# A graph layer on one core: the source table's rows made inside the first level's steps, the node layer in one matmul per batch with its inputs fetched at the batch's own step

## The chip, the cores and the metric

The kernel runs on one core of one Trainium2 chip. A core has five engines with queues of their own: TensorE (PE in the profile, with its weight loads as PEld), VectorE (DVE), ScalarE (ACT), GpSimd (POOL) and SyncE (SP), which here only issues transfers. The metric is the device time of one execution in microseconds. Three executions of the kernel before took 2367.4, 2370.09 and 2371.28 us; the median is 2370.09 us.

## The reference, cut to what matters

```python
h = relu(layernorm(x))                                   # x: 12500 nodes x 64
e = silu(concat(h[src], h[dst], w) @ eW1 + eb1)          # 212500 edges x 128, dst is sorted
e = silu(e @ eW2 + eb2)
agg = segment_sum(e, src, 12500)                         # 12500 x 128
out = x + silu(concat(h, agg) @ nW1 + nb1) @ nW2 + nb2   # 12500 x 64
```

The sum goes over `src`, while the list is sorted by `dst`. `h[src] @ eW1[:64]` is a row of a table A, with one row of 128 numbers per node, and `h[dst] @ eW1[64:128]` a row of a table B. `h @ nW1[:64]` is called the own rows' part of the node layer below.

## The kernel before, in words

The 12500 nodes stand in 100 buckets of 125, and four buckets are a batch (25 batches). The 212500 edges come in 208 blocks of 1024.

**Feed.** `normed` makes h, `turned` transposes four buckets of it (tile `hr`), and `products` multiplies them by both halves of eW1 (`product`, L246, L250, L253: matmul, copy on ACT, difference on DVE, since every table row is kept as a rounded half and a rest). Table A goes to DRAM as `ta` (tile `rows_a`), table B as `tb` (tile `got`), and the turned rows as `hd`. The feed is a list of small pieces, handed out between other work.

**Sends.** For every block the B rows of its 1024 edges are picked by matmul (L493) from a window of `tb`, copied on ACT into `qs` (L505, eight buffers) and scattered to DRAM rows in `q` by eight indirect transfers on POOL (L515), four for each half block. The rows' places come from counting on DVE (L426, L434, L451, L453) and PE (L439, L463, in the PSUM tile `misc`); `picked` (L415) makes the selection matrix.

**Levels.** Each bucket's rows of `q` are filled in ranks. When the blocks up to a level's end are scattered, its ranks are full in every bucket, and a level of 25 batches can run; there are 14 levels, and the last needs all blocks. A step (512 edges; one step to a batch in the first two and the last eight levels, two in the others) is: `one` on DVE (L644, which node each edge has), its transpose (L601, L606), the rows of `q` and A added (L615, L622) and SiLU (L631), the second layer (L655, L661, L665), the sum over nodes (L675) and its addition to `aggT` (L684 or L686). A batch's `qt` (rows of `q`) is fetched four batches ahead (L569) and its `a` (rows of `ta`) three ahead (L589), both on SP's queue; the first `qt` of a level waits for the scatters.

**Node layer.** In the last level `nodes` follows each batch in four parts, one at each free place of the step after: four z matmuls (two on the sums, L312; two on the turned rows, L315) and SiLU (L317); four matmuls into `o` (L321); the sum with x into `os` on DVE (L324); the store (L326 through the helper at L126). Its inputs `xr` (L126, and an addition on POOL, L300) and `hrn` (L302) are issued with the batch's `qt`, four batches ahead. `os` and `zs` have two buffers each, the inputs six.

**Order.** PE, DVE, ACT and SP run in the order in which the code is written. `turn` is the list of a step's parts with four places (None) between, at which a planner (numbers PLAN_...) puts pieces of sends and the feed, to keep scatters ahead of POOL. The first eight blocks go out before that loop, with four pieces of the feed to each piece of a block; then 39 pieces of blocks with three pieces of the feed each; then the loop over the steps.

Of the kernel before, what the change touches and what calls it, by code (L numbers as in the profile page):

```python
# [50 lines left out]
G = 4  # L51
# [13 lines left out]
PLAN_AHEAD, PLAN_ROOM = 30.0, 36.0  # L65
# [14 lines left out]
def tile_gnn(ctx: ExitStack, tc: tile.TileContext, x, src, dst, ew, eW1, eb1, eW2, eb2, nW1, nb1, nW2, nb2, out):  # L80
# [112 lines left out]
    nodes_i = const.tile([P, L], I32, name="nodes_i")  # L193
# [3 lines left out]
    diff = const.tile([P, P], I32, name="diff")  # L197
# [3 lines left out]
    for a in range(2):  # L201
        half = slice(a * D, (a + 1) * D)
        nc.gpsimd.dma_start(w1[half, :, :], eW1[: 2 * D, :].rearrange("(s k) f -> k s f", s=2))
    same = const.tile([P, 1], F32, name="same")
# [33 lines left out]
    def product(s, hr, ps, tag, to):  # L238
# [13 lines left out]
        for a in range(2):  # L252
            nc.vector.tensor_tensor(to[:, a, 1], abs_[a], to[:, a, 0], op=OP.subtract)  # L253

    hd = dram.tile([P, NB // 2, P], F32, name="hd")
    bkt = const.tile([P, 2 * TB, NP], BF16, name="bkt")
# [39 lines left out]
    def nodes_in(B, sb):  # L296
# [4 lines left out]
        hr = sb.tile([P, G // 2, P], F32, name="hrn")  # L301
        nc.sync.dma_start(hr, hd[:, b // 2 : b // 2 + G // 2, :])  # L302
        return xr, hr

    def nodes(B, xr, hr, ps, sb, tag):

        b = B * G

        zs = sb.tile([P, 2, G // 2, L], F32, name="zs")
        z = [ps.tile([P, G // 2, L], F32, name="z", tag=tag) for _ in range(2)]  # L310
        for a in range(2):
            nc.tensor.matmul(z[a], w1g, aggT[:, b + a : b + G : 2, :], start=True, stop=False)  # L312
        for a in range(2):
            half = slice(a * D, (a + 1) * D)
            nc.tensor.matmul(z[a], w1n[half, :], hr[half, :, :L], start=False, stop=True)  # L315
        for a in range(2):
            nc.scalar.activation(zs[:, a], z[a], AF.Silu, bias=nb1c)  # L317
        yield
        o = ps.tile([L, G, D], F32, name="o", tag=tag)
        for t in range(G):  # L320
            nc.tensor.matmul(o[:, t, :], zs[:, t % 2, t // 2, :], w2n, start=True, stop=True)  # L321
        yield
        os_ = sb.tile([L, G, D], F32, name="os")
        nc.vector.tensor_tensor(os_, o, xr, op=OP.add)  # L324
        yield
# [9 lines left out]
    with ExitStack() as work:  # L335
# [8 lines left out]
        misc = sgp.tile([P, 2 * NB + L], F32, name="misc")  # L344
        upto, numbers, spots = misc[:, :NB], misc[:, NB : 2 * NB], misc[:, 2 * NB :]
        nc.tensor.matmul(upto, before, none, start=True, stop=True)
# [131 lines left out]

        def send(s):
# [56 lines left out]
        def send_all(s0, s1):  # L536

            for s in range(s0, s1):
# [5 lines left out]
                for j, _ in enumerate(itertools.zip_longest(send(s), count(s + 1))):  # L544
                    if s + 1 == nblocks and j == 1:
                        counted(s)
# [573 lines left out]
```

## Time and profile before

| what | value |
|---|---|
| median of three executions | 2370.09 us |
| the profiled execution | 2367.31 us, span 2365.5 us |
| busy: PE, PEld, DVE, ACT, POOL | 2028.7, 1902.7, 1814.7, 1333.0, 1655.9 us |
| mean granted clock of TensorE | 0.892 |
| scatters | 1661, mean 973 ns |
| moved by the transfers | 572.83 MB |

A row of the timeline gives the start (us from the span's start), the busy time, the engine, the line, the operation and its tiles, how many are merged, and in brackets how long the engine had been idle and what ended that. An engine with a trailing q is its queue: SPq rows are transfers being issued. A row of the windows gives the stretch, its length, and for each engine the busy time with the number of instructions, then the granted clock of TensorE as a share of full speed, the busy share of the transfer engines and GB/s.

### The profile page before, as it was taken

How to read it: one execution, taken by the hardware profiler on the slowest of the kernel's cores; microseconds unless marked ns; L12 is line 12 of the kernel's file. 1: busy time of each engine (PE TensorE's matmuls, PEld its weight loads, DVE VectorE, ACT ScalarE, POOL GpSimd, SP SyncE). 2: the span in 40 equal slices, each digit the busy share in tenths (PEclk: the TensorE clock that was granted, in tenths of full speed). 3: DMA queues.
4: the chain of work that ended last, by engine and by line, in shares of the span. 5: the costliest groups of instructions: out<-in, count | busy, mean ns of one | idle time of the engine just before them, and what ended most of it. 6: DMA issues, size and time to landing. Idle time of an engine off the chain costs nothing.

```text
span 2365.5 us, 47589 instructions
## 1 busy us (share of the span) xinstructions
PE 2028.7 (86%) x16818; PEld 1902.7 (80%) x16818; DVE 1814.7 (77%) x2865; ACT 1333.0 (56%) x2966; POOL 1655.9 (70%) x1724
## 2 busy tenths in 40 slices
PE   4667798952599779969995999999999999989997
PEld 2455697942499669959995999999999999989885
DVE  8899788885488868886886888888888888875221
ACT  3334464631277547737773777666666666656542
POOL 5777777777777777777777777777777777776110
PEclk9655597965699879979996999999999999999998
DMA  5566797964488647867884888888888888878662
GB/s 161 188 235 231 268 298 248 324 225 133 155 297 263 224 170 250 264 197 255 288 286 143 284 280 265 268 276 271 285 267 291 274 275 277 272 244 277 196 196 85
DMA packets 239835, 572.83 MB, mean 242 GB/s; under 512 B 46756, under 2 KB 99072, under 8 KB 239177
## 3 DMA queue, kind: packets, MB, share of 16 engines
q1 hardware_dynamic: 155283, 390.76, 51.5%
q0 software_dynamic: 54112, 124.65, 14.4%
q10 hardware_dynamic: 30196, 54.31, 7.3%
q8 instruction: 136, 2.23, 0.4%
q14 instruction: 108, 0.88, 0.1%
HBM read 356.61 MB, written 212.87 MB: 241 GB/s over the span
## 4 chain that ended last, share of the span: by engine, by line
PE 58%; DMA 12%; DVE 11%; POOL 6%; issue 4%; ACT 2%; SPq 2%; POOLq 0%; DVEq 0%; ACTq 0%
PE seg L675 15%; PE p L661 14%; PE pt L622 10%; DMA q<-qs,to 8%; PE pt L615 6%; POOL q L515 6%; PE qp L493 6%; PE lr L601 4%; DMA out_dram<-os 3%; DVE each L434 1%; DVE oh L426 1%; PE bc L379 1%; DVE rank L453 1%; DVE terms L451 1%; DVE pick L415 1%
## 5 line engine op out<-in xcount | busy, mean ns | idle before, releaser
L515 POOL DMA_INDIRECT q<-qs,to x1661 | 1616.1, 973 | 526.5 <-issue 396.9
L631 ACT ACTIVATE e<-pt 128x512 f32<-128x512 f32 x450 | 268.7, 597 | 496.2 <-PE pt L622 495.2
L675 PE MATMUL seg<-one,e 128*128 128x125 f32 x3600 | 502.3, 283 | 2.0 <-DVE aggT L686 1.7
L661 PE MATMUL p<-w,e 128*128 128x128 f32 x3600 | 498.6, 282 | 0.0
L661 PEld LDWEIGHTS p<-w,e 128*128 128x128 f32 x3600 | 449.9, 195 | 9.9 <-issue 9.2
L675 PEld LDWEIGHTS seg<-one,e 128*128 128x128 f32 x3600 | 444.2, 193 | 9.4 <-issue 4.9
L622 PE MATMUL pt<-oneT,a 125*128 125x128 f32 (+1 forms) x2800 | 423.0, 289 | 14.4 <-DMA a<-ta 8.5
L493 PEld LDWEIGHTS qp<-win,pick 128*128 128x128 f32 x1664 | 268.5, 224 | 202.6 <-ACT qs L505 121.6
L493 PE MATMUL qp<-win,pick 128*128 128x256 f32 x1664 | 347.7, 340 | 93.5 <-ACT qs L505 60.6
L505 ACT COPY qs<-qp 128x512 f32<-128x512 f32 x418 | 245.1, 587 | 323.9 <-DMA q<-qs,to 222.9
L622 PEld LDWEIGHTS pt<-oneT,a 125*128 125x128 f32 x2800 | 356.8, 194 | 18.3 <-issue 9.7
L644 DVE TENSOR_TENSOR one<-misc,qt 128x500 f32<-128x500 f32 x450 | 302.4, 672 | 78.1 <-PE seg L675 42.1
L686 DVE TENSOR_TENSOR aggT<-aggT,seg 128x500 f32<-128x500 f32 x325 | 218.4, 672 | 185.9 <-PE seg L675 182.2
L434 DVE TENSOR_REDUCE each<-oh 128x100 bf16<-128x800 bf16 x208 | 321.0, 1543 | 7.2
L615 PE MATMUL pt<-ident,qt 128*128 128x128 f32 x1800 | 276.3, 277 | 10.4 <-ACT qs L505 10.1
L606 ACT CAST oneT<-lr 125x512 fp32r<-125x512 f32 x450 | 265.5, 590 | 13.2 <-PE lr L601 13.2
L665 ACT ACTIVATE e<-p 128x512 f32<-128x512 f32 x450 | 268.7, 597 | 6.1 <-PE p L661 6.1
L655 ACT COPY p<-b2f 128x512 f32<-128x512 f32 x450 | 267.2, 594 | 0.0
L451 DVE TENSOR_TENSOR terms<-oh,misc 128x800 f32<-128x800 bf16 x208 | 203.6, 979 | 38.2 <-PE misc L439 38.2
L615 PEld LDWEIGHTS pt<-ident,qt 128*128 128x128 f32 x1800 | 215.3, 144 | 19.7 <-ACT qs L505 11.0
L453 DVE TENSOR_REDUCE rank<-terms 128x8 f32<-128x864 f32 x208 | 219.0, 1053 | 7.2
L426 DVE TENSOR_TENSOR oh<-misc,bkt 128x800 bf16<-128x800 f32 (+1 forms) x209 | 203.8, 975 | 2.4 <-ACT bkt L831 2.4
(153 smaller groups left out, 1653.4 us busy)
## 6 DMA issues: line engine op xcount, KB each, us to landing
a<-ta SPq DMA_DIRECT2D x350, 512.0 KB
qt<-q SPq DMA_DIRECT2D x250, 288.0 KB
qt<-q SPq DMA_DIRECT2D x100, 576.0 KB
q<-zeros ACTq DMA_DIRECT2D x25, 1080.0 KB
q<-qs,to POOLq DMA_INDIRECT x1661
win<-tb SPq DMA_DIRECT2D x208, 120.0 KB
tb<-got SPq DMA_DIRECT2D x30, 512.0 KB
q<-zeros ACTq DMA_DIRECT2D x20, 720.0 KB
```

Source lines behind the costliest of these rows:

```text
L434: nc.vector.tensor_reduce(each, oh.rearrange("p t b -> p b t"), AX.X, OP.add)
L493: nc.tensor.matmul(qp[:, t % 2, :k], halves(pick[:, t * P : (t + 1) * P]), halves(win[:, :k, v]), start=v == 0, stop=v == 1,)
L515: ins = nc.gpsimd.indirect_dma_start(out=q[:], out_offset=bass.IndirectOffsetOnAxis(ap=to[:k, j : j + 1], axis=0), in_=qs[:k, t % 2, a, :] ...
L606: nc.scalar.copy(halves(oneT), st[k].pop("lr"))
L615: nc.tensor.matmul(pt[:, t, :], qt[:, j, :H], ident, is_transpose=True, start=t == 0, stop=False, skip_group_check=True)
L622: nc.tensor.matmul(pt[:, cols, :], halves(a[:L, b, i * H : (i + 1) * H]), halves(oneT[:, cols, :]), start=False, stop=i == 1, skip_group_c ...
L631: nc.scalar.activation(e1, pt, AF.Silu)
L644: nc.vector.tensor_tensor(one.rearrange("p (b j) l -> p b j l", j=n), spots[:, None, None, :].to_broadcast(wide), loc[:, tiles[0][1] : til ...
L655: nc.scalar.copy(p2, b2f)
L661: nc.tensor.matmul(p2[:, t, :], e1[:, t, :], w2, start=False, stop=t == G - 1, skip_group_check=True)
L665: nc.scalar.activation(e2, p2, AF.Silu)
L675: nc.tensor.matmul(item[2][:, b, :], e2[:, t, :], one[:, t, :], start=j < G, stop=j >= G * (n - 1))
```

## The change

1. The feed makes no table A. `hd` is stored earlier in a group, and table B's tile has three buffers to itself. Six pieces of a group become four, and the first eight blocks get three pieces of the feed to each piece of a block.
2. In the first level a batch's `a` is not loaded. `made_a` loads the four buckets' turned rows from `hd` (128 KB), waits three free places, makes A straight into the tile `a` and stores it to `ta` for the later levels. It also makes the own rows' part (two matmuls, two copies on ACT) and stores it to a new DRAM tensor `own` (250 KB a batch).
3. The planner takes 2.6 us more for each step of the first level.
4. The node layer has one z matmul over 500 columns. It accumulates onto the own rows' part, which is copied by DVE into `misc`, the counters' PSUM tile, no longer needed then. In the last level `one` reads the node numbers from SBUF, since `misc` is overwritten.
5. `xr` and the own rows' part (`zo`) are issued at the batch's own step instead of four batches ahead, with five buffers; `zs` and `os` have three. The first `qt` of the last level is issued three batches ahead instead of four, two at once.
6. After the last step the parts left are written in an order of their own (`ending`). The check for irregular input (`flagged`) is computed after the last block, not after the node layers.

```diff
-        z = [ps.tile([P, G // 2, L], F32, name="z", tag=tag) for _ in range(2)]
...
+        if bank is not None:
+            nc.tensor.matmul(bank, w1g, sums, start=False, stop=True, skip_group_check=True)
+            nc.scalar.activation(zsv, bank, AF.Silu, bias=nb1c)
...
         os_ = sb.tile([L, G, D], F32, name="os")
         nc.vector.tensor_tensor(os_, o, xr, op=OP.add)
+        for more in then:
+            nc.vector.tensor_copy(bank, more())
...
-            while B not in done_a:
-                next(feed)
             a = lda.tile([P, G, 2 * H], F32, name="a")
-            nc.sync.dma_start(a, ta_buckets[:, B * G : B * G + G])
+            if c == 0:
+                making[B] = made_a(B, a)
+                next(making[B])
+            else:
+                nc.sync.dma_start(a, ta_buckets[:, B * G : B * G + G])
...
+        def made_a(B, a):
...
+            hr = late.tile([P, G // 2, P], F32, name="hrl")
+            nc.sync.dma_start(hr, hd[:, B * G // 2 : (B + 1) * G // 2, :])
+            for _ in range(3):
+                yield
+            yield from product(0, hr, mm, "mm", a.rearrange("p g (k h) -> p g k h", k=2))
+            yield
+            nc.sync.dma_start(ta_buckets[:, B * G : B * G + G], a)
+            zo = [mm.tile([P, G // 2, L], F32, name="zo", tag="mm") for _ in range(2)]
+            for h in range(2):
+                half = slice(h * D, (h + 1) * D)
+                nc.tensor.matmul(zo[h], w1n[half, :], hr[half, :, :L], start=True, stop=True)
+            zos = late1.tile([P, G * L], F32, name="zos")
+            for h in range(2):
+                nc.scalar.copy(zos.rearrange("p (i a l) -> p i a l", a=2, l=L)[:, :, h], zo[h])
+            yield
+            nc.sync.dma_start(own[:, B, :], zos)
...
+            if c == len(LEVELS) - 1:
+                node_in[B] = nodes_in(B, ndp[0])
             if g == n - 1:
-                fetch(c * (NB // G) + B + NQ)
+                i = c * (NB // G) + B
+                while len(fetched) <= i + NQ and (len(fetched) < final or i + 3 >= final):
+                    fetched.append(0)
+                    fetch(len(fetched) - 1)
...
-            rows_a = fp.tile([P, G, 2, H], F32, name="rows_a", tag="rows")
-            yield from product(0, hr, mm, "mm", rows_a)
             nc.sync.dma_start(hd[:, b // 2 : (b + G) // 2, :], hr)
...
-                for _ in range(2 if i < PIECES else 4):
+                for _ in range(2 if i < PIECES else 3):
...
+        ending = [(s_add, -2), (s_seg, -1), None, None, (s_add, -1), None, None]
...
-                            for name, bufs in (("nd_in", NQ + 2), ("nd", 2)):
+                            for name, bufs in (("nd_in", NQ + 1), ("nd", 3)):
```

In the last level SP's queue changes as follows. A batch's rows on SP, before (`out_dram` is the store of `os`; what is named in brackets is waited for, with DMAHW an earlier transfer of the same ring place):

```order
L126 DMA xr<-in_x_dram 112x256 [waits DMAHW3_49,DVE_49]
L126 DMA xr<-in_x_dram 13x256 [waits DMAHW4_49]
L302 DMA hrn<-hd 128x256 [waits DMAHW5_49,PE_49]
L589 DMA a<-ta 128x1024 [waits DMAHW6_49]
L126 DMA out_dram<-os 112x256 [waits DMAHW7_49]
L126 DMA out_dram<-os 13x256 [waits DMAHW0_49]
L569 DMA qt<-q 128x576 [waits DMAHW1_49]
```

And with the change:

```order
L126 DMA xr<-in_x_dram 112x256 [waits DMAHW7_49,Pool_49]
L126 DMA xr<-in_x_dram 13x256 [waits DMAHW0_49]
L304 DMA zo<-own 128x500 [waits DMAHW1_49]
L588 DMA qt<-q 128x576 [waits DMAHW2_49,PE_49]
L608 DMA a<-ta 128x1024 [waits DMAHW3_49,PE_49]
L126 DMA out_dram<-os 112x256 [waits DMAHW4_49,DVE_49]
L126 DMA out_dram<-os 13x256 [waits DMAHW5_49]
```

The wait for DVE has moved from the load of `xr`, which stood ahead of the store, to the store itself; the load waits for POOL.

The same steps on PE, before, from the rows-and-A part of one step to the second node matmul (`z` and `o` are the node layer, `p` the second edge layer):

```order
L615 MATMUL pt<-ident,qt 128x128 x4
L622 MATMUL pt<-oneT,a 128x128 x8
L312 MATMUL z<-aggT,w1g 128x250 x2
L315 MATMUL z<-hrn,w1n 128x250 x2
L661 MATMUL p_29205<-w_196,e_29183 128x128 x4
L321 MATMUL o<-w2n,zs 125x64 x4
```

And with the change:

```order
L661 MATMUL pt<-ident,qt 128x128 x4
L668 MATMUL pt<-oneT,a 128x128 x8
L315 MATMUL misc<-aggT,w1g 128x500
L712 MATMUL p_29346<-w_198,e_29330 128x128 x4
L325 MATMUL o<-w2n,zs 125x64 x4
```

The two matmuls on the turned rows are gone from the last level.

In the first level PE had this before, from the sum over nodes of one step to the next:

```order
L675 MATMUL seg<-one,e_2639 128x125 x4
L615 MATMUL pt<-ident,qt 128x128 x4
L622 MATMUL pt<-oneT,a 128x128 x8
L661 MATMUL p_2688<-w_196,e_2682 128x128 x4
L493 MATMUL qp<-win_184,pick 128x256 x4
```

And with the change (`ab` is A's product, `zo` the own rows' part, `qp` belongs to the sends):

```order
L247 MATMUL ab<-w_140,hrl 128x128 x4
L726 MATMUL seg<-one,e_2563 128x125 x4
L510 MATMUL qp<-win_187,pick 128x256 x4
L386 LDWEIGHTS sel_190
L386 MATMUL bc<-rowsD,sel_190 128x512
L661 MATMUL pt<-ident,qt 128x128 x4
L668 MATMUL pt<-oneT,a 128x128 x8
L627 MATMUL zo<-hrl,w1n 128x250 x2
```

The step has `ab` and `zo` besides. In both kernels 46 half blocks are sent ahead of the first step. In the 24 steps from there PE then sends 24 half blocks before the change, eight of them at the end in one piece, and 33 with it, one or two to a step; by step 47 both have sent 120, and from there to the last level the orders are alike. The last seven half blocks ahead of the first step have no piece of the feed between them in the changed kernel.

More of the change, by code (lines that the diff above doesn't have):

```diff
@@ L300, in nodes_in, with nodes @@
         nc.gpsimd.tensor_tensor(xr, xr, nb2b[:L, None, :].to_broadcast([L, G, D]), op=OP.add)
[L301 to L305, printed above, removed]
+        zo = sb.tile([P, G * L], F32, name="zo")
+        nc.sync.dma_start(zo, own[:, B, :])
+        return xr, zo
+    def nodes(B, xr, zo, ps, sb, tag, bank=None, then=()):
         b = B * G
-        zs = sb.tile([P, 2, G // 2, L], F32, name="zs")
-        z = [ps.tile([P, G // 2, L], F32, name="z", tag=tag) for _ in range(2)]
[L311 to L317, printed above, removed]
+        sums = aggT[:, b : b + G, :].rearrange("p t l -> p (t l)")
+        zs = sb.tile([P, G, L], F32, name="zs")
+        zsv = zs.rearrange("p t l -> p (t l)")
+        if bank is not None:
+            nc.tensor.matmul(bank, w1g, sums, start=False, stop=True, skip_group_check=True)
+            nc.scalar.activation(zsv, bank, AF.Silu, bias=nb1c)
+        else:
+            z = ps.tile([P, G * L], F32, name="z", tag=tag)
+            nc.tensor.matmul(z, w1g, sums, start=True, stop=True)
+            nc.vector.tensor_tensor(zo, z, zo, op=OP.add)
+            nc.scalar.activation(zsv, zo, AF.Silu, bias=nb1c)
         yield
```

85 lines of the change are left out of this document (50 added, 35 removed).

## The prediction

> **What bounds the kernel now.** I read the page first (busy times and slices), then the scatters' line, then the timeline of POOL at the start and of the last level.
>
> ```profile
> PE 2028.7 (86%) x16818; PEld 1902.7 (80%) x16818; DVE 1814.7 (77%) x2865; ACT 1333.0 (56%) x2966; POOL 1655.9 (70%) x1724
> POOL 5777777777777777777777777777777777776110
> ```
>
> Rows: busy time, share and instructions; then POOL's busy tenths in 40 slices of 59.1 us. No engine is at 90%, and POOL stands at 7 in every slice from the second to the 36th. That is its ceiling:
>
> ```profile
> L515 POOL DMA_INDIRECT q<-qs,to x1661: 905/969/1905, 42.2 to 2173.3; - x185
> POOL q L515 <- issue: 396.9, 1302, 0.3
> ```
>
> A scatter takes 0.97 us, and in 1302 cases 0.30 us pass before the next for no reason the profile shows: 1.273 us each. From the first (42.2 us) to the last (2173.3) are 1660 intervals; at 1.273 they make 2113 us of the 2131. So POOL lost about 18 us in all, and what starts later than the scatters allow is seen in the levels, whose first fetch waits for them. The time is the scatters' end plus the last level. Both ends of that stretch can be moved.
>
> At the start POOL ran dry, because the pieces of the feed stood ahead of the sends:
>
> ```profile
> 51.02 0.97 POOL L515 DMA_INDIRECT q<-qs,to  x1 [3.11 <-ACT hr L725]
> 68.18 0.97 POOL L515 DMA_INDIRECT q<-qs,to  x1 [1.79 <-ACT qs L508]
> 92.30 0.96 POOL L515 DMA_INDIRECT q<-qs,to  x1 [2.98 <-ACT qs L508]
> 126.13 0.96 POOL L515 DMA_INDIRECT q<-qs,to  x1 [2.73 <-ACT got L250]
> ```
>
> The four idle times less 0.30 us each make 9.4 us.
>
> In the last level (25 steps, a node layer behind each) two things set the step. First PE's work, in the first steps, where nothing waits:
>
> ```profile
> 2196.00 0.60 PE L615 MATMUL pt<-ident,qt 128*128 128x128 f32 x4
> 2199.41 0.60 PE L615 MATMUL pt<-ident,qt 128*128 128x128 f32 x4
> 2200.69 1.06 PE L312 MATMUL z<-aggT,w1g 128*128 128x250 f32 x4
> 2201.68 0.69 PE L315 MATMUL z<-hrn,w1n 64*128 64x250 f32 x4
> 2202.30 1.16 PE L661 MATMUL p<-w,e 128*128 128x128 f32 x8
> 2203.30 0.98 PE L321 MATMUL o<-w2n,zs 128*125 128x64 f32 x8
> 2205.30 0.60 PE L615 MATMUL pt<-ident,qt 128*128 128x128 f32 x4
> ```
>
> Rows are start, busy time, line. A step without a node layer takes 2199.41 − 2196.00 = 3.41 us, the first one with it 2205.30 − 2199.41 = 5.89. The own rows' matmul (L315) holds PE from 2201.68 to 2202.30: 0.62 us. Later the step is longer:
>
> ```profile
> 2313.16 0.42 DVE L324 TENSOR_TENSOR os<-o,xr 125x256 f32<-125x256 f32 x1 [3.83 <-DMA out_dram<-os]
> 2313.61 0.77 SPq L126 DMA_DIRECT2D xr<-in_x_dram  x2
> 2315.34 0.87 SPq L126 DMA_DIRECT2D out_dram<-os  x2
> 2319.43 0.42 DVE L324 TENSOR_TENSOR os<-o,xr 125x256 f32<-125x256 f32 x1 [4.68 <-DMA out_dram<-os]
> DVE os L324 <- DMA out_dram<-os: 84.3, 18, 5.7
> ```
>
> VectorE finishes `os` at 2313.58; SP, which had stood at the load of `xr` because that buffer is free only then, issues it at 2313.61, then `hrn` and `a`, and only at 2315.34 the store of the step before. It lands some 4 us later, at 2319.43, and only then has the next `os` a buffer. One turn, 2313.16 to 2319.43, is 6.27 us, longer than PE's 5.89. VectorE runs in order, so the sums into `aggT` and with them the next z come late. Over the level:
>
> ```profile
> 2332.16 0.60 PE L615 MATMUL pt<-ident,qt 128*128 128x128 f32 x4
> 2353.00 0.43 DVE L324 TENSOR_TENSOR os<-o,xr 125x256 f32<-125x256 f32 x1 [3.72 <-PE o L321]
> SPq L985 <- DVE flag_i L984: 0.2, 1, 0.2
> ```
>
> From the step at 2199.41 to the last at 2332.16 are 21 steps, 132.75 us, 6.32 each; from there to the last `os` 21.3 us.
>
> **The change part by part.**
>
> *The last level's steps.* The load of `xr` now reuses a buffer whose `os` lies several steps back, so SP does not stop at it ahead of the store; three result buffers give the store a step more. The turn through VectorE, SP and the store is broken. PE's step loses L315: 5.89 − 0.62 = 5.27 us. One matmul over 500 columns stands for two over 250, the same columns, so I cost that at nothing (bounds ±0.1 us, the overlap of L312's 1.06 us with the row after it). What is late next? VectorE gains a copy of 128x500 into `misc` (0.67 us by the nearest row of that size, L644 below), standing between `os` and the next `aggT`. A step's VectorE work is then 0.67 + 0.67 + 0.43 + 0.67 = 2.44 us of 5.27. The one buffer `misc` goes round through z (1.0), the second layer (1.0), `o` (0.8), `os` (0.43) and the copy (0.67): about 4.1 us with the gaps, under 5.27. SP still issues seven transfers a step. 21 × (6.32 − 5.27) = 22.1 us. Ends: 0 if the stores or loads still set 6.3, 24 if z comes 0.1 us cheaper too.
>
> *The end.* Four node layers lie behind the last step: 4 × 0.62 = 2.5 us less; the last sum over nodes moves ahead of a node layer that it stood behind (about 0.9 us less on the chain), and one copy into `misc` comes onto it (0.67 more). Gain 2.7 us. The early check saves the chain nothing to speak of: SP had to wait 0.2 us for it.
>
> *Inputs of the node layer.* `zo` is 250 KB where `hrn` was 128. A step of the last level moves 288 + 512 + 125 + 250 + 125 = 1300 KB; in 5.27 us that is 247 GB/s. The stretch 2100 to 2175 below moved 285. I cost it at nothing; the inputs are issued two steps ahead of their use, some 10 us.
>
> *The first `qt` of the last level* comes one step later in the order, and POOL's end was at 2174.3. PE had then no stall; 0 to +2 us.
>
> *The feed without A.* Rows: lines with busy time and mean; then windows.
>
> ```profile
> L434 DVE TENSOR_REDUCE each<-oh 128x100 bf16<-128x800 bf16 x208 | 321.0, 1543 | 7.2
> L426 DVE TENSOR_TENSOR oh<-misc,bkt 128x800 bf16<-128x800 f32 (+1 forms) x209 | 203.8, 975 | 2.4 <-ACT bkt L831 2.4
> L453 DVE TENSOR_REDUCE rank<-terms 128x8 f32<-128x864 f32 x208 | 219.0, 1053 | 7.2
> L451 DVE TENSOR_TENSOR terms<-oh,misc 128x800 f32<-128x800 bf16 x208 | 203.6, 979 | 38.2 <-PE misc L439 38.2
> L415 DVE SCALAR_TENSOR_TENSOR pick<-bc,same,extra 128x512 fp32r<-128x512 f32 x208 | 154.0, 740 | 14.1 <-PE bc L379 13.0 <-DMA extra<-ewR 1.2
> L644 DVE TENSOR_TENSOR one<-misc,qt 128x500 f32<-128x500 f32 x450 | 302.4, 672 | 78.1 <-PE seg L675 42.1 <-DMA qt<-q 17.4 <-PE misc L439 15.9
> L253 DVE TENSOR_TENSOR rows_a<-ab,rows_a 128x256 f32<-128x256 f32 x50 | 19.0, 416 | 5.7 <-ACT rows_a L250 5.5
> L250 ACT CAST rows_a<-ab 128x256 fp32r<-128x256 f32 x50 | 17.0, 374 | 30.8 <-PE ab L246 22.7 <-issue 5.0 <-ACT qs L508 1.6
> L246 PE MATMUL ab<-w,hr 64*128 64x128 f32 x432 | 77.8, 450 | 23.7 <-DVE got L253 10.7 <-ACT hr L725 7.2 <-ACT qs L505 4.6
> L493 PE MATMUL qp<-win,pick 128*128 128x256 f32 x1664 | 347.7, 340 | 93.5 <-ACT qs L505 60.6 <-DVE pick L415 15.9 <-DVE rows_a L253 6.9
> ```
>
> ```profile
> 100.00:200.00 100.00, 69.56 (x319) 52.47 (x319) 92.25 (x165) 38.48 (x111) 74.30 (x76) 0.52 0.63 221
> 300.00:377.00 77.00, 69.63 (x606) 66.73 (x606) 69.24 (x105) 46.70 (x105) 58.46 (x61) 0.93 0.87 286
> 500.00:600.00 100.00, 33.63 (x121) 23.89 (x120) 65.72 (x99) 16.30 (x47) 75.92 (x80) 0.50 0.44 141
> 2100.00:2175.00 75.00, 75.00 (x701) 74.25 (x700) 50.86 (x86) 48.78 (x107) 56.60 (x59) 1.00 0.88 285
> ```
>
> The windows' columns are PE, PEld, DVE, ACT, POOL, clock.
>
> The feed loses 19.0 us of VectorE, 17.0 of ACT, 25/54 of L246's 77.8 on PE (432 records, 8 to a product). In 100 to 200 us VectorE was 92% busy: it sets the pace there. A group of four buckets had six pieces with two products in them and now has four with one; to the three pieces of a block came 12 pieces of the feed and now come 9. That is 4 products a block before and 2.25 now, 1.75 × 2 × 0.416 = 1.5 us of VectorE less, and a quarter of a group's normalization more: about 1 us a block spared. Eight blocks are worth 8 us against gaps of 9.4. I take 6: the first gap lies in the start itself, where nothing is removed. Ends: −2 (other pieces now stand in a bad place) to +9.4. POOL has no idle time later, so what it wins here goes through to the last scatter, and with it to the gates of the levels.
>
> *A and the own rows in the first level.* Each step gets on VectorE 0.83 us, on ACT four copies of some 0.37 (1.5 us), on PE the product (8 records of 0.18: 1.44 us, most of them measured at half clock) and `zo` (0.62): 25 times 2.06 us, 52 us of PE at most.
>
> ```profile
> 484.03 0.60 PE L615 MATMUL pt<-ident,qt 128*128 128x128 f32 x4
> ```
>
> The cover is the hole behind the second level, 500 to 600 us, where PE is 34% busy because the next level waits for scatters. It is wide enough: the last step ahead of it stands at 484.03, and 52 us later it is 536. If that cover were gone, the 52 us would come out at the third level's start.
>
> What must not happen is that POOL runs dry meanwhile:
>
> ```profile
> 0.00:280.00 280.00, 56.09 (x184) 43.03 (x184) 0.64 0.63 215
> 0.00:280.00 280.00, 174.69 (x176) 0.64 0.63 215
> ```
>
> By 280 us, where the first step stood, PE had done 184 / 4 = 46 half blocks and POOL 176 / 4 = 44: a lead of 2 × 5.09 = 10 us. Now seven half blocks without feed stand ahead of it; VectorE needs 5.3 us a block for the five counting lines above, some 2.7 a half block, and POOL 5.09, so the lead grows by up to 7 × 2.4 = 17 us, less some 10 for the three products that PE makes in a row there. I reckon with 15 to 20. In the level a step sends 33 / 24 = 1.375 half blocks, 7.0 us of POOL. Its VectorE work is 0.67 + 0.67 + 0.83 + 1.375 × 2.65 = 5.8 us, its PE work 3.41 + 2.06 + 1.375 × 0.84 = 6.6. Both stay under 7.0, PE narrowly. Cost taken: nothing; ends 0 to +15.
>
> *SP's queue in the first level.* Per step `hrl`, `ta` and `own` instead of `a`; `ta` waits for VectorE's differences and `own` for ACT, and the windows for sends stand behind them, two blocks (20 us) ahead of need. Hidden.
>
> **Sum.** 2367.3 − 22.1 − 2.7 − 6.0 = 2336.5 us for the profiled execution. Its 2367.3 lies 2.8 us under the median of the runs shown (2370.1), so I say 2339.
>
> **Rivals.**
>
> *The first level starves POOL* (the other side). PE's 6.6 us hold at full clock. In 100 to 200 us the clock was 0.52 with PE 70% busy; in 300 to 377, with PE 90% busy, 0.93. If the new waits (products on copies, `zo` on PSUM places) keep the clock at half, a step is about 12 us, 5 late, 24 steps 120 us, less a lead of 17: 103 us later, 2442. It decides from 7.0 + (17 + 31) / 24 = 9.0 us a step. For it speaks the narrow margin, against it that PE had 90% in the same level and gets more to do. The Trainium skill ("TensorE: Matmul & The Clock Gate", section on the HAM clock gate) says that a window of about 3.4 us in which PE idles halves the clock and a busy one restores it. By that rule a step too slow at half clock would keep PE busy and be raised again, so that 2442 could not last; the rows of 300 to 377 agree with the busy side.
>
> *The last level stays with its transfers.* The step stays at 6.3 because stores and loads come late at a higher rate: 2339 + 22 = 2361. For it: at 2319.43 the wait is on a store. Against: that store was issued late, not slow.
>
> *The early gaps stay.* POOL gains nothing: 2345.
>
> **Chances.** Forecast 0.60; early gaps stay 0.18; last level stays 0.10; POOL starved a little, gain halved (2355) 0.03; starved past 9.0 us a step 0.06; other ways to no change 0.03. Faster by over 0.2% (about what a measurement of this kernel can tell) 0.90, within 0.2% 0.03, slower 0.07. The range 2326 to 2354 goes from all gaps gone (−9.4, not −6), 24 us in the steps and 4 us more, to a last level that keeps two thirds of its wait or a first level that costs 15.
>
> **What would show it.** Right: steps of 5.2 to 5.4 us in the last level; no wait of `os` for stores; no gap of over 1 us on POOL after 60 us; the last scatter at about 2167; a hole before the third level that is some 50 us shorter. Wrong: POOL idle between 280 and 450, waiting for ACT's copies; a half clock there; z waiting for the copy into `misc`; `os` waiting for stores.

## The result, and the profile after

The changed kernel takes 2340.35 us (median of four runs, 2336.79 to 2341.64) against 2370.69 us for the kernel before on the same chip. The ratio is 0.9868, with a 95% interval from 0.9847 to 0.9889: 1.3% less time, the interval clear of 1, and 1.4 us from the 2339 that was forecast. The profiled execution took 2336.79 us, with a span of 2334.9 us against 2365.5.

The page of the changed kernel, in the order in which the page of before was read: busy time of the engines, POOL's slices, and the answer on the scatters' line with its idle time.

```profile
PE 2016.0 (86%) x16768; PEld 1886.7 (81%) x16768; DVE 1831.2 (78%) x2890; ACT 1345.5 (58%) x2991; POOL 1658.7 (71%) x1724
POOL 5777777777777777777777777777777777777110
...
L532 POOL DMA_INDIRECT q<-qs,to x1661: 903/972/1902, 41.5 to 2166.9; - x185
```

POOL is at its ceiling from the second slice on, as before. The first scatter starts at 41.5 us and the last at 2166.9: 2125.4 us, where 1660 intervals of 1.273 make 2113. POOL loses 12 us in all; before it was 18.

Of the four early idle times the timeline of POOL between 40 and 160 us has these two left that are over 0.6 us:

```profile
49.20 0.97 POOL L532 DMA_INDIRECT q<-qs,to  x1 [2.00 <-ACT hr L779]
...
75.59 0.96 POOL L532 DMA_INDIRECT q<-qs,to  x1 [0.66 <-ACT qs L525]
```

The last level, by PE's rows of its first, its fourth and its last step, then by SP's and VectorE's rows in one of its steps:

```profile
2186.63 0.60 PE L661 MATMUL pt<-ident,qt 128*128 128x128 f32 x4
...
2196.84 0.60 PE L661 MATMUL pt<-ident,qt 128*128 128x128 f32 x4
...
2306.47 0.60 PE L661 MATMUL pt<-ident,qt 128*128 128x128 f32 x4
```

```profile
2222.69 1.03 SPq L126 DMA_DIRECT2D out_dram<-os  x2
2223.83 0.77 SPq L126 DMA_DIRECT2D xr<-in_x_dram  x2
...
2326.46 0.42 DVE L328 TENSOR_TENSOR os<-o,xr 125x256 f32<-125x256 f32 x1 [4.35 <-issue]
```

The 21 steps with a node layer take 2306.47 − 2196.84 = 109.63 us, 5.22 each, against 132.75. SP issues the store first and the load of `xr` behind it, and no `os` of the level waits for a store. The last `os` ends at 2326.88, 20.4 us behind the start of the last step (21.3 before), and the span ends 8.0 us after it (12.1 before).

So the 30.6 us between the two spans come from these places:

| place | before | after | gain |
|---|---|---|---|
| last scatter starts | 2173.3 | 2166.9 | 6.4 |
| first step of the last level | 2189.2 | 2186.6 | 2.6 |
| its 21 steps with a node layer | 132.75 | 109.63 | 23.1 |
| from the last step to the end of the last `os` | 21.3 | 20.4 | 0.9 |
| from there to the end of the span | 12.1 | 8.0 | 4.0 |

The last four rows make up the 30.6. The first row stands beside that path. The level before the last waits for scatters, and its first step starts at 2097.7 us before and at 2091.2 with the change, 6.4 us earlier. From there PE works without a break, before (75.00 of 75 us in the window that the prediction shows) as with the change:

```profile
2091.00:2138.00 47.00, 47.00 (x438) 46.35 (x437) 39.83 (x61) 30.89 (x69) 35.71 (x38) 1.00 0.87 284
```

Of these 6.4 us, 3.9 are lost before the last level starts. They go in one step of the level before it. Two windows of the changed kernel there (PE, PEld, VectorE, ACT, POOL, clock, DMA, GB/s), PE's rows, and VectorE's between the same times:

```profile
2138.00:2142.10 4.10, 1.94 (x18) 1.71 (x15) 2.52 (x11) 1.89 (x7) 3.19 (x4) 0.97 0.86 258
2142.10:2146.00 3.90, 3.83 (x23) 3.86 (x24) 1.01 (x4) 1.07 (x2) 2.98 (x4) 0.60 0.43 164
```

```profile
2137.85 0.60 PE L661 MATMUL pt<-ident,qt 128*128 128x128 f32 x4
...
2142.17 0.37 PE L491 MATMUL turned<-ident,s 128*1 128x128 f32 x1 [2.23 <-DVE s L489]
2142.34 1.92 PE L712 MATMUL p<-w,e 128*128 128x128 f32 x8
...
2145.80 0.60 PE L661 MATMUL pt<-ident,qt 128*128 128x128 f32 x4
2147.08 1.11 PE L712 MATMUL p<-w,e 128*128 128x128 f32 x8
```

```profile
2139.98 0.25 DVE L479 TENSOR_TENSOR u<-misc,zone 1x100 f32<-1x100 f32 x1 [1.25 <-PE misc L470]
...
2141.89 0.14 DVE L489 TENSOR_TENSOR s<-bad 128x1 f32<-128x1 f32 x1
```

The flag is made at once behind the last block's counting. Its turn through PE (L491) needs `s`, and `s` stands on VectorE behind a chain of nine small operations from 2139.98 on. PE stands for 2.23 us, then runs at half clock for a while (`p` takes 1.92 us where the next one takes 1.11), and the step takes 2145.80 − 2137.85 = 7.95 us where the same step took 4.05 before.

In the first level POOL did not run dry. Windows of the changed kernel: PE's L510 and POOL's L532 alone up to the first step of that level, then all engines during the level, and the hole of before:

```profile
0.00:258.00 258.00, 55.14 (x188) 42.67 (x188) 0.62 0.55 183
```

```profile
0.00:258.00 258.00, 164.47 (x165) 0.62 0.55 183
```

```profile
257.00:447.00 190.00, 162.54 (x1197) 140.87 (x1197) 140.37 (x233) 105.20 (x265) 144.80 (x149) 0.88 0.75 248
```

```profile
500.00:600.00 100.00, 62.13 (x438) 53.71 (x436) 84.56 (x132) 37.53 (x91) 76.21 (x79) 0.72 0.72 237
```

At 258 us PE has made 188 / 4 = 47 half blocks and POOL has sent 165 / 4 = 41: a lead of 29 us, not the 10 of before. From its first step to its last the level then takes 189 us, 7.9 us a step (118 us and 4.9 before), and POOL is busy for 144.8 / 190 = 76% of it, which is its ceiling. The window from 500 to 600, the hole of before with 34% of PE, now has 62%.

### The profile page after: what moved, and what is told of

It is laid out like the page before. It is cut to its first block, busy times and chain, and to the rows that moved or that the text cites. A ratio compares the mean times of both kernels' runs of the same rounds, so it can differ in the third digit from the quotient of the medians.

```text
span 2334.9 us, 47675 instructions
## 1 busy us (share of the span) xinstructions
PE 2016.0 (86%) x16768; PEld 1886.7 (81%) x16768; DVE 1831.2 (78%) x2890; ACT 1345.5 (58%) x2991; POOL 1658.7 (71%) x1724
## 3 DMA queue, kind: packets, MB, share of 16 engines
q8 instruction: 136, 2.23, 0.4%
## 5 line engine op out<-in xcount | busy, mean ns | idle before, releaser
L532 POOL DMA_INDIRECT q<-qs,to x1661 | 1618.1, 974 | 518.9 <-issue 395.6
L726 PE MATMUL seg<-one,e 128*128 128x125 f32 x3600 | 507.7, 285 | 1.9 <-DVE aggT L737 1.5
L712 PEld LDWEIGHTS p<-w,e 128*128 128x128 f32 x3600 | 454.3, 196 | 21.1 <-issue 20.4
L668 PE MATMUL pt<-oneT,a 125*128 125x128 f32 (+1 forms) x2800 | 426.8, 290 | 12.1 <-DMA a<-ta 6.5
L510 PE MATMUL qp<-win,pick 128*128 128x256 f32 x1664 | 338.4, 332 | 60.0 <-ACT qs L522 38.7
L510 PEld LDWEIGHTS qp<-win,pick 128*128 128x128 f32 x1664 | 260.9, 218 | 140.6 <-ACT qs L522 73.7
L737 DVE TENSOR_TENSOR aggT<-aggT,seg 128x500 f32<-128x500 f32 x325 | 218.8, 673 | 185.9 <-PE seg L726 179.8
L695 DVE TENSOR_TENSOR one<-misc,qt 128x500 f32<-128x500 f32 x425 | 285.7, 672 | 78.0 <-PE seg L726 42.7
```

The lines of the kernel that those rows point to most:

```text
L510: nc.tensor.matmul(qp[:, t % 2, :k], halves(pick[:, t * P : (t + 1) * P]), halves(win[:, :k, v]), start=v == 0, stop=v == 1,)
L532: ins = nc.gpsimd.indirect_dma_start(out=q[:], out_offset=bass.IndirectOffsetOnAxis(ap=to[:k, j : j + 1], axis=0), in_=qs[:k, t % 2, a, :] ...
L668: nc.tensor.matmul(pt[:, cols, :], halves(a[:L, b, i * H : (i + 1) * H]), halves(oneT[:, cols, :]), start=False, stop=i == 1, skip_group_c ...
L695: nc.vector.tensor_tensor(one.rearrange("p (b j) l -> p b j l", j=n), (spots if c < len(LEVELS) - 1 else nodes1)[:, None, None, :].to_broa ...
L712: nc.tensor.matmul(p2[:, t, :], e1[:, t, :], w2, start=False, stop=t == G - 1, skip_group_check=True)
L726: nc.tensor.matmul(item[2][:, b, :], e2[:, t, :], one[:, t, :], start=j < G, stop=j >= G * (n - 1))
```

## Experiments

Twelve runs were made, of ten kernels, in three lots. The kernels of a lot shared a chip and the runs of the kernel before. The first and the third lot came to chips on which every kernel, the one before too, took about 1.5 times as long. From those lots only the parts are read that run there as on the other chip: the last level and the end, where the steps agree to a hundredth of a microsecond, and the level before the last after its sends are done.

**The flag.** First lot. Two kernels move it, one to where it was before and one eight steps on by the traces (the two texts on it say six and seven).

```diff
                         counted(s)
-                        flagged()
...
+        nc.vector.tensor_tensor(s, bad[:, 0:1], bad[:, 1:2], op=OP.add)
+        nc.tensor.transpose(fp, s, ident)
+        nc.vector.tensor_reduce(m, fp, AX.X, OP.max)
+        nc.vector.tensor_copy(flag_i, m)
     flag = nc.values_load(
```

> The changed kernel with the flag's chain of two VectorE operations, a transpose and a reduction put back to the end of the program. Theory: the 3.9 us that the next-to-last level loses in one step belong to the place of the flag's transpose, right behind the last block's counting: that level then has no step of 7.9 us, the last level's first step stands at about 2182.7 us instead of 2186.6, and the end behind the last `os` is about 12 us instead of 8.0, so that the total stays at 2340 (2337 to 2343). Rival (the long step is the clock's, not the flag's): the step stays, the end gets 4 us longer, 2344. Second rival (the early check never shortened the end): the end stays 8 us and the total is 2336.

```diff
                         counted(s)
-                        flagged()
...
         for k in range(first, len(steps) + 1):
+            if k == len(steps) - 30:
+                flagged()
```

> The changed kernel with the flag made six steps later in the same level, when the last block's counting has long been done. Theory: the transpose then waits for one short VectorE operation at most, the level loses under 1 us there, the end keeps its 8 us: 2336.5 (2335 to 2338). Rival (any transpose that waits for VectorE costs a level the same): 2340.

The ratios to the kernel before, 0.9893 (0.9825 to 0.996) and 0.9859 (0.9782 to 0.9936), are too wide to tell these apart, and the level with the long step is disturbed on that chip. Yet that one step takes 3.92 us in both traces, and 6.36 and 6.41 in the two other kernels of the lot, which leave the flag in its place. The end is not disturbed. The last `os` of each, flag at the end first (span 3427.8 us), flag late second (span 3456.9):

```profile
3415.36 0.43 DVE L328 TENSOR_TENSOR os<-o,xr 125x256 f32<-125x256 f32 x1 [3.96 <-issue]
```

```profile
3448.41 0.42 DVE L328 TENSOR_TENSOR os<-o,xr 125x256 f32<-125x256 f32 x1 [3.96 <-issue]
```

With the flag at the end 3427.8 − 3415.79 = 12.0 us follow the last `os`, with the early flag 3456.9 − 3448.83 = 8.1. So an early flag does shorten the end; the rival by which it never did is out. By how much differs: in all traces here 12.0 to 12.1 us follow the last `os` in the four kernels that make the flag at the end, and 5.8 to 8.3 in the others.

Second lot, on an undisturbed chip, with the changed kernel beside it:

> The changed kernel as it is, on the same chip as the three beside it, as their yardstick. Expected: 2340 us (2336 to 2343), 0.987 of before, with one step of 7.9 us in the next-to-last level.

> The changed kernel with the flag made seven steps later in the same level. Theory: the long step of 7.9 us becomes 4.05 and the step that holds the transpose now is at most 3.6, so that the last level starts 3.8 us earlier and the total is 3.5 to 4 us under that of the changed kernel beside it, 2336. Rival (the last level's start does not hang on that step): no difference, 2340.

The changed kernel took 2337.49 us (2332.03 to 2338.4), ratio 0.9857 (0.9842 to 0.9872); with the late flag it took 2334.21 us (2333.37 to 2335.4), ratio 0.985 (0.9837 to 0.9864). The 3.3 us between the medians are less than the 6.4 us between the fastest and the slowest run of the changed kernel, so the traces decide. The steps in question, PE's rows of the changed kernel first, then of the kernel with the late flag, there with the flag's turn through PE and the first step of the last level:

```profile
2138.16 0.60 PE L661 MATMUL pt<-ident,qt 128*128 128x128 f32 x4
2146.32 0.60 PE L661 MATMUL pt<-ident,qt 128*128 128x128 f32 x4
...
2187.16 0.60 PE L661 MATMUL pt<-ident,qt 128*128 128x128 f32 x4
```

```profile
2138.82 0.60 PE L660 MATMUL pt<-ident,qt 128*128 128x128 f32 x4
2142.87 0.60 PE L660 MATMUL pt<-ident,qt 128*128 128x128 f32 x4
...
2170.09 0.27 PE L491 MATMUL turned<-ident,s 128*1 128x128 f32 x1
2170.20 0.60 PE L660 MATMUL pt<-ident,qt 128*128 128x128 f32 x4
...
2183.81 0.60 PE L660 MATMUL pt<-ident,qt 128*128 128x128 f32 x4
```

8.16 us became 4.05, the turn through PE costs 0.11 us where it stands now, and the last level starts 3.35 us earlier although POOL's last scatter came 1.5 us later in this run. So that start hangs on PE's steps and not on the last scatter. By the traces the place of the flag cost 4 us, and the theory holds. This kernel has the lowest median of all that ran.

**What broke the turn in the last level.** The change does two things to it: it loads the inputs at the batch's own step, so that SP no longer stops ahead of the store, and it adds a third result buffer. Three kernels take them apart. The changed kernel with two buffers (first lot):

```diff
-                            for name, bufs in (("nd_in", NQ + 1), ("nd", 3)):
+                            for name, bufs in (("nd_in", NQ + 1), ("nd", 2)):
```

> The changed kernel with two result buffers instead of three. Theory: the order on SP alone broke the turn; a store lands some 4 to 5 us after its issue, two steps are 10.4 us, so steps stay at 5.2 us and the total at 2340 (2338 to 2343). Rival: the third buffer is what breaks it; steps go back to 6.2 or so, 21 us more, 2361.

The kernel before with the inputs at the own step alone (second lot); the two lines stand in the fetch of the batch, four batches ahead (the texts of this run and the next say one), in the one place and at its step in the other:

```diff
-            if c == len(LEVELS) - 1:
-                node_in[B] = nodes_in(B, ndp[0])
...
+            if c == len(LEVELS) - 1:
+                node_in[B] = nodes_in(B, ndp[0])
             if g == n - 1:
```

> The kernel before with one edit: the node layer's inputs (xr and the last node rows) are loaded at the batch's own step instead of one batch earlier, so that SP does not stop at the load of xr ahead of the store; two result buffers stay, the own rows' matmul stays. Theory: the turn through VectorE, SP and the store is gone, the last level's step is PE's 5.89 instead of 6.32, 21 x 0.43 = 9 us, 2361. Rival (the store's landing with two buffers sets the step whatever SP's order): 2370.

The kernel before with the third buffer alone (third lot):

```diff
-                            for name, bufs in (("nd_in", NQ + 2), ("nd", 2)):
+                            for name, bufs in (("nd_in", NQ + 2), ("nd", 3)):
```

> The kernel before with one edit: three result buffers instead of two, the node layer's inputs still loaded one batch earlier, so that SP still stops at the load of xr ahead of the store. Theory: one turn through VectorE, SP and the store may now span two steps, 6.27 us against 11.8, so the step is 5.89 again and the total 2358 (2356 to 2361), as with the inputs alone. Rival (SP's stop at xr delays the store whatever the buffers): the step stays at 6.3 us and the total at 2369.

PE's rows of the fourth and the last step of the level, in this order of kernels:

```profile
3297.19 0.60 PE L661 MATMUL pt<-ident,qt 128*128 128x128 f32 x4
...
3406.83 0.60 PE L661 MATMUL pt<-ident,qt 128*128 128x128 f32 x4
```

```profile
2199.05 0.60 PE L613 MATMUL pt<-ident,qt 128*128 128x128 f32 x4
...
2322.81 0.60 PE L613 MATMUL pt<-ident,qt 128*128 128x128 f32 x4
```

```profile
3395.04 0.60 PE L615 MATMUL pt<-ident,qt 128*128 128x128 f32 x4
...
3518.88 0.60 PE L615 MATMUL pt<-ident,qt 128*128 128x128 f32 x4
```

The 21 steps take 109.64, 123.76 and 123.84 us. The third buffer adds nothing to the changed kernel. On the kernel before, either edit alone brings the step from 6.32 to 5.89 us, PE's own length there. With two buffers the order on SP must be right; with three a store may be late by a step. The kernel with the inputs alone took 2357.1 us (2356.2 to 2362.2), ratio 0.995 (0.9935 to 0.9965): 12 us under the kernel before, of which 9.0 are in these steps by the traces; the interval, 8 to 15 us, holds both. The one with three buffers has a ratio of 0.996 (0.9927 to 0.9992).

**The own rows.** The changed kernel with the own rows' matmul back in the last level, in the first lot and again in the third. The copy into `misc` and the making of the own rows' part in the first level go with it; the rest is kept:

```diff
-            z = ps.tile([P, G * L], F32, name="z", tag=tag)
-            nc.tensor.matmul(z, w1g, sums, start=True, stop=True)
-            nc.vector.tensor_tensor(zo, z, zo, op=OP.add)
+        for a in range(2):
+            nc.tensor.matmul(z[a], w1g, aggT[:, b + a : b + G : 2, :], start=True, stop=False)
+        for a in range(2):
+            nc.tensor.matmul(z[a], w1n[half, :], hr[half, :, :L], start=False, stop=True)
...
-                nc.tensor.matmul(zo[h], w1n[half, :], hr[half, :, :L], start=True, stop=True)
...
-            nc.sync.dma_start(own[:, B, :], zos)
```

> The changed kernel with the own rows' matmul back in the last level's steps (two matmuls over 250 columns each for the nodes' part and the own rows' part, no own rows' part kept in DRAM, no copy into the bank), late inputs and three result buffers kept, A in the first level kept. Theory: a step is 5.22 + 0.62 = 5.85 us, 21 x 0.62 = 13 us, and 2.5 us in the four node layers of the end, so 2356 (2352 to 2359); the first level is up to 0.6 us a step shorter, which the hole ahead of the third level swallows. Rival (the matmul is hidden behind another wait, and the step was set by the turn alone): 2341. Second rival (the turn comes back with the longer chain): 6.3 us a step, 2363.

> The changed kernel with the own rows' matmul back in the last level (as own_back above), A in the first level, late inputs and three result buffers kept. Theory: a last-level step is 5.89 instead of 5.21 us, 21 x 0.68 = 14.3 us; the end behind the last step is as long as with the change (20.2 us on the other chip), not 2.5 us longer; the last scatter stays at about 2166. Total 14 us over the changed kernel, 2352 (2349 to 2355). If the first level's own rows were what made its steps long, the first level is shorter and the lead of the sends larger, with nothing to show for it in the end. Rival (the own rows' work in the first level delays the scatters): the last scatter is 2 to 5 us earlier than 2166 and the total 2348.

PE's rows of the second run (the fourth and the last step), and its last `os`:

```profile
3359.52 0.60 PE L649 MATMUL pt<-ident,qt 128*128 128x128 f32 x4
...
3483.28 0.60 PE L649 MATMUL pt<-ident,qt 128*128 128x128 f32 x4
```

```profile
3503.09 0.42 DVE L326 TENSOR_TENSOR os<-o,xr 125x256 f32<-125x256 f32 x1 [2.88 <-PE o L323]
```

The steps take 123.76 us in both runs, 14.1 more than with the change, 0.67 each; the rivals (hidden; or the turn back at 6.3) are out. The end, from the last step to the end of the last `os`, is 20.2 us with the own rows' matmul in it, against 19.8 to 21.0 in the kernels without it: the 2.5 us of the first text are not there. As for the whole kernel, 0.9869 (0.9801 to 0.9938) and 0.9887 (0.9849 to 0.9926) leave the 14 us open on these chips; what is known of them comes from the steps.

**The first level.** The planner reckons with 2.6 us of PE's time for what a step of the first level has more. One kernel takes that away (second lot):

```diff
-PLAN_AHEAD, PLAN_ROOM, PLAN_FIRST = 30.0, 36.0, (2.6, 0.0)
+PLAN_AHEAD, PLAN_ROOM, PLAN_FIRST = 30.0, 36.0, (0.0, 0.0)
```

> The changed kernel with the planner's allowance for the first level's work on PE (2.6 us a step) set to nought, so that its order puts fewer half blocks ahead of and between the first level's steps. Theory (the first level's work is carried by the lead that the sends have on POOL, and that lead is used up to 5 us): POOL runs dry in the first level for some 10 to 40 us, the last scatter is late by as much, 2350 to 2380. Rival (PE's order there does not matter, since VectorE and ACT hand on as they come): 2340.

Its median is 2368.4 us (nine runs from 2363.5 to 2371.2, and one of 3990.3, which the ratio leaves out), the ratio 0.9992 (0.9982 to 1.0002): the whole gain of the change is gone. PE's order in the level is then again that of the kernel before, with eight half blocks in one piece towards its end. Waits of POOL between 280 and 420 us (in total, times, longest), a row of POOL there, and the window of the level with all engines:

```profile
POOL q L532 <- ACT qs L525: 34.7, 11, 5.7
```

```profile
333.30 0.97 POOL L532 DMA_INDIRECT q<-qs,to  x1 [5.75 <-ACT qs L525]
```

```profile
257.00:435.00 178.00, 149.73 (x1147) 129.17 (x1148) 112.52 (x189) 98.39 (x242) 111.55 (x116) 0.88 0.70 236
```

POOL waits for rows 11 times, 34.7 us, is busy 63% of the level instead of 76, and its last scatter comes at 2199.1, 33 us after that of the changed kernel beside it (2165.6). The steps of the level are shorter than with the change (178 us by the window, 178 / 24 = 7.4 each), and still the time is lost: a step that holds fewer sends is not what counts, sends that come in time are.

**The early gaps.** Third lot: four pieces of the feed behind each piece of a send, as before the change, and two.

```diff
-                for _ in range(2 if i < PIECES else 3):
+                for _ in range(2 if i < PIECES else 4):
```

> The changed kernel with four pieces of the feed behind each piece of a send in the first blocks, as before the change, instead of three; the pieces themselves stay without A. Theory of the prediction (VectorE's work for the feed set the early gaps): the rate of the feed's work per block comes back to near that of before, POOL's loss between 60 and 260 us goes from 4 us back to 8 to 11, the last scatter to 2170 to 2173, total 2341 to 2344. Rival (it was A's own operations that stood in the way, not the number of pieces): the loss stays at 4 us, 2338.

```diff
-                for _ in range(2 if i < PIECES else 3):
+                for _ in range(2):
```

> The changed kernel with two pieces of the feed behind each piece of a send in all of the first blocks. Theory: the loss between 60 and 260 us goes from 4 us to 1 or 2, but more of the feed is left over for the first level's loop, which then starts later and with the sends behind that much rest: a gain of 2 us at the most (2336), a loss of 10 us if the rest of the feed holds up the sends there (2348). Rival (the pieces' number has no part in it): 2338.

Both are inconclusive. On that chip POOL lost, between 60 and 260 us, 39 us with four pieces, 35 with two and 31 in the kernel with the own rows back (three pieces), by one trace each. The changed kernel lost 4 elsewhere, so the chip's own loss is far larger than the 4 to 7 us in question. Ratios: 0.9878 (0.982 to 0.9936) and 0.9894 (0.9833 to 0.9955).

## Why the prediction was right

*The last level's steps* (−22.1 forecast, −23.1 measured): right in both parts. The turn was worth 9.0 us (132.75 to 123.76 with SP's order alone), as 21 × 0.43 said. The own rows' matmul was worth 14.1, not 13.0: one matmul over 500 columns was cheaper than the two over 250 (0.89 us to PE's next row, where the two took 0.99), so that a step lost 0.67 us and not 0.62. The forecast had left that open by 0.1 us. The copy into `misc`, seven transfers a step at 1300 KB and the third buffer changed nothing there: PE is busy for 120.92 of the level's 121 us.

*The early gaps* (−6.0 forecast): the last scatter came 6.4 us earlier, at 2166.9 for a forecast of about 2167. The gaps that ended at 68, 92 and 126 us went as said. That it was A's work on VectorE, and not the smaller number of pieces, that opened them was only argued, and the two runs meant for it did not tell. VectorE is 96% busy between 100 and 200 us with the change (92% before), and POOL 76.5%, its ceiling. The feed is done sooner, and the first level starts at 257.8 us instead of 279.7.

*The path* ("the scatters' end plus the last level"): right in size, not as a mechanism. The last level starts behind PE's steps, 15.9 us after the last scatter before, 19.7 with the change and 16.7 with the late flag. What POOL won came through at the start of the level before it.

*A and the own rows in the first level* (nothing, up to +15): right in the result, and the reason holds. But two sizes on the way were off. The lead at the level's start was 29 us, where 15 to 20 were reckoned, and a step took 7.9 us, where 6.6 were. PE's busy time in the window is 162.5 / 24 = 6.8 us a step, so the work was about right; what was left out is 1.1 us a step of waiting, with the clock at 0.88. Both errors had opposite signs. Seen in the rows of PE and POOL, the lead went down to 5 us at the end of the level:

```profile
440.32 0.72 PE L510 MATMUL qp<-win,pick 128*128 128x256 f32 x4
```

```profile
445.97 0.97 POOL L532 DMA_INDIRECT q<-qs,to  x1 [0.30 <-ACT e L716]
```

The rival on the other side, POOL starved, was thus nearer than its 6 in 100 made it look: with the planner's allowance gone POOL did starve, at 7.4 us a step and not at the 9.0 reckoned. The bound of 9.0 took the order as given, and it is the order that decides how much lead there is to use. The rival's half clock had no part in it: the windows of the level give 0.88 with the change and without the allowance alike. The Trainium skill ("TensorE: Matmul & The Clock Gate", section on the HAM clock gate), by which a busy window restores the clock, agrees.

*The hole before the third level* took the longer level, as forecast: 62% of PE between 500 and 600 us where 34% had been.

*The first `qt` of the last level* (0 to +2): nothing was lost. The level begins 3.4 us behind the last step of the level before it in both kernels.

*The end* (−2.7 forecast, −0.9 measured): this step failed. Its terms were 2.5 us for four matmuls L315, 0.9 for the order of the last steps, and 0.67 given back for a copy into `misc`. The order came out: with L315 put back the end is 20.2 us, 1.0 under that of before. The 2.5 did not come out. From the z of one node layer to the z of the next the changed kernel takes 4.64, 5.75 and 4.02 us, and 4.72 from the last z to the end of its `os`. With L315 put back the same stretches are 5.30, 6.41, 3.25 and 3.99. So the matmul is saved in the first two, 0.66 us each. Behind them no step lies between the layers any more, and the last z has to wait for the copy into the one buffer `misc`:

```profile
2322.16 1.50 PE L315 MATMUL misc<-aggT,w1g 128*128 128x500 f32 x2 [1.16 <-DVE misc L330]
2324.43 1.94 PE L325 MATMUL o<-w2n,zs 128*125 128x64 f32 x8 [0.77 <-ACT zs L316]
```

This is the round through `misc` that the prediction put at 4.1 us and hid under a step of 5.27. It is 4.02 us, and at the end nothing hides it. Behind these waits the clock fell to half, too: the last z takes 1.50 us and the last `o` 1.94, where the layer before takes 1.01 and 1.08, and the stretch to the end of `os` is 4.72 us instead of 3.38. These 1.3 us are most of the 1.8 that are missing. The same stretch is 4.1 to 5.3 us in the other kernels that keep this end. In the two with L315 put back the clock stays full until the last `os` is done.

*The early flag* ("saves the chain nothing to speak of: SP had to wait 0.2 us for it"): this failed twice, with opposite signs. Every engine reads the flag at the end, and the row quoted was SP's wait for it. What hung on the flag was POOL: once it has read it, POOL ends its queue with a drain of 6.93 us. The drains (min, median and longest in ns, first and last start) and SP's last wait, before and with the change:

```profile
L1116 POOLq DRAIN x3: 50/109/6928, 2357.8 to 2365.2; - x3
...
SPq L1116 <- PEq L1116: 4.8, 2, 4.2
```

```profile
L1163 POOLq DRAIN x3: 50/109/6928, 2312.5 to 2334.7; - x3
...
SPq L1163 <- PEq L1163: 0.7, 2, 0.5
```

Before, the drain ran from 2357.8 to 2364.7. SP had seen the last stores land and was done at 2360.6, and then stood 4.2 us until POOL was done (the view puts this down to PE's queue, which had drained at 2358.9). With the change POOL had the flag in time and drained from 2312.5 on, under the last node layers. Only the landing of the last stores still stands behind the last `os`: 8.0 us to the end instead of 12.1. And the place to which the flag went cost 3.9 us, since PE had to wait for it there. The prediction did not ask whether the change adds a wait at that place. The two cancel, and that was luck. So the sum came out at 2336.5 for a profiled 2336.79 although the steps were 1.0 us better than forecast, the end 1.8 worse, and the flag left out with +3.9 and −4.0.

## What to carry to other kernels

A queue that runs in order should never meet a load that waits for a buffer ahead of a store that something else waits for. Here either the order or one more buffer cured it, and both together brought no more than one. A small operation that turns through an in-order engine (here one 128x1 transpose) costs what the engine waits for its input, not its own 0.3 us: it belongs some steps behind the chain that feeds it. A check at the end of a program belongs ahead of the last stage, so that the engines can end their queues (here POOL's drain of 6.93 us) under other work. A buffer that goes round unseen under a long step has to be counted anew where the steps run out. Work that is moved under a cover needs its allowance in whatever plans the order: the same work, in the same level, cost nothing with it and 31 us without.

## What the runs showed of the hardware that was not expected

PE's clock fell to half behind a wait of 2.23 us, in a window of 4.1 us in which PE was busy for 1.94, and stayed there for most of the next 3.9 us (0.60 in the window). It fell again in the changed kernel's last node layers, where no wait was longer than 1.16 us:

```profile
2319.40:2322.80 3.40, 1.72 (x10) 1.25 (x10) 1.01 (x2) 0.47 (x1) 0.00 (x0) 0.99 0.10 30
2322.80:2326.20 3.40, 2.63 (x10) 1.76 (x8) 0.00 (x0) 0.68 (x1) 0.00 (x0) 0.50 0.05 15
```

PE was busy for 1.72 of 3.40 us there, and the next 3.40 us ran at half. In the 3.40 us before, it had been busy for 2.27 and the clock stayed full. The Trainium skill ("TensorE: Matmul & The Clock Gate", section on the HAM clock gate) gives about 3.4 us of idle time for it; here windows that were half idle were enough.

Two of the chips ran all kernels 1.47 to 1.5 times as long (3495 and 3557 us for the kernel before, against 2369). The changed kernel itself did not run there; the kernels one edit away from it had ratios of 0.986 to 0.989, where it has 0.986 and 0.987 elsewhere. Steps with no sends beside them took exactly as long as elsewhere (3.40 us, and 5.22 and 5.89 in the last level), and a scatter took the same 0.97 us. Steps with sends took up to 13 us instead of 4.05. Waits of two kinds in the changed kernel with two result buffers there (in total, times, longest):

```profile
POOL q L532 <- ACT qs L525: 1082.4, 185, 17.4
...
ACT e L677 <- remote: 313.9, 46, 19.5
```

ACT (and VectorE, for 285.8 us at L737) waits there for matmuls whose rows in the trace had ended some microseconds before, and the releaser is often not in the records. What held the signals up is open.
